# Local attention layers: when GpSimd takes and initialises the value buffers of a tile

## The chip, the cores and the metric

The kernel runs on one core of one Trainium2 chip. The metric is the device time of one execution in microseconds (us), median over several runs. The core has five engines with one queue of instructions each, all in order: TensorE (PE in the profile; PEld is its weight loads), VectorE (DVE), ScalarE (ACT), GpSimd (POOL) and SyncE (SP, which here only issues DMA transfers; its queue is written SPq).

## The reference, cut to what matters

A sequence of blocks works on `x` of 4 x 512 x 128 numbers: cross attentions, mixtures of experts, a feed-forward net, and in the middle a local transformer of six layers. The change lies in the attention of those six layers:

```
for i in range(DEPTH):                                  # DEPTH = 6
    x = attn_layer(shift_tokens(x), Wqkv[i], q_scale[i], k_scale[i], Wo[i]) + x
    x = ffn_layer(shift_tokens(x), ...) + x
# attn_layer: q, k, v = split(x @ Wqkv); 16 heads of 64
#   q = l2norm(q) * qs;  k = l2norm(k) * ksc;  rotary tables on both
#   each window of 32 tokens attends to itself and to the window before it
#   attn = softmax(8 * q k^T, masked);  out = attn @ v;  return out @ Wo
```

The queries and keys are multiplied by the inverse of their norms ("inverse norms" below). The values are not normalised.

## The kernel before, in words

**Tiles and periods.** In `local_transformer` the work is cut into 96 tiles of 128 tokens: 6 layers x 4 sequences (`b`) x 4 tiles (`tt` = 0 to 3). The loop at L2095 runs one period for each `n`. In one period three tiles are worked on at different stages: `T` (number n) gets its queries and keys, their rotation and norms and its values; `T1` (n-1) gets its transposes (`turned`), scores and softmax; `T2` (n-2) gets its probabilities transposed, its average over the values, its output product and its residual. A feed-forward row `F` of the layer is threaded through as well, one quarter per period. The order is written out by hand: the block runs under `manual_schedule`, so each engine executes its instructions in the order of the code; semaphores make it wait where another engine's result is needed.

**GpSimd's queue in one period** is, in order: the sums of the rotation, `rotate` L1865 (four of 128x512, one for each half of the queries and of the keys), with `turned`'s copy of the key edge (L1892, or the memset L1894 at tt = 0) between the second and the third; then `normalise`: L1875, after which ScalarE does a logarithm and an exponential (L1876, L1877), then L1878 to L1881 on 128x32, then L1884, four products of 128x512 with the inverse norms; and then, in `values(T, 0)`, the initialisation of the value buffers L1913, at tt = 0 also L1915 and L1916. In some periods more stands in the queue: two small instructions for the feed-forward's moments (L551, L552), six instructions that build the next layer's tables (L1792, L1798, in the last period of each layer but the last), and two memsets at n = 4 (L527, L528, in `clear`).

**Values.** `values` at L1905 holds two buffers for each tile, `v1` and `v2` (both `v` in the profile), from a pool of three buffers for each name (L1812). Both are 128 x 2 x 8 x 65: 64 numbers for each head, and a 65th column that is one in `v1`, so that the average's product also gives the softmax denominator. GpSimd writes the ones (L1913, 16 numbers per partition). At tt = 0 there is no window before the first, so GpSimd also clears two blocks of 32 partitions of `v2` (L1915, L1916). TensorE multiplies the tokens by the value weights (L1919), and ScalarE copies each half from PSUM to `v1` (L1920, columns 0 to 63). `v2` is `v1` moved by 32 partitions: SyncE issues four DMA copies for each tile (L1922, L1926, L1927, L1928), and two more at tt > 0 which fetch the window before from the previous tile's `v1` (L1924, L1930). These copies move the column of ones too.

`average` (L1980) reads `v1` and `v2` of tile n in period n+2, in two halves g = 0 and 1. So the buffers of tile n-3 have their last reader in period n-1, at `average(T2, 1)`.

Of the kernel before, what the change touches and what calls it, by code (L numbers as in the profile page):

```python
# [21 lines left out]
F32 = mybir.dt.float32  # L22
# [13 lines left out]
DEPTH, LH, LD, WIN = 6, 16, 64, 32  # L36
# [236 lines left out]
def tile_kernel(ctx: ExitStack, tc: tile.TileContext, A: dict, out: bass.AP):  # L273
    nc = tc.nc
    V, G, SC, PE, DMA = nc.vector, nc.gpsimd, nc.scalar, nc.tensor, nc.sync
# [40 lines left out]
    def p_mm(*shape):  # L316
        return psum(shape, "mm", 2)

    def p_tr(*shape):
        return psum(shape, "tr", 2)  # L320
# [199 lines left out]
    def clear(pool, i):  # L520


        t = pool.tile([128, NT, D], F32, name="xn")
        t = t.rearrange("p a b -> p (a b)")[:, : 2 * ROW].rearrange("p (a b) -> p a b", b=ROW)

        def fill(e):
            e.memset(t, 0.0)  # L527
            e.memset(t[:, 1, D + 1 :], NOWHERE)  # L528

        def send(e):  # L530
            for j in (1, 2) if i else (0,):
                r = sent[j].rearrange("(c p) d -> p c d", p=128)
                e.dma_start(r, bc(t[:, int(j != 1)], [128, r.shape[1], ROW], 1))

        def send_back(e):
            r = back[i].rearrange("(c p) d -> p c d", p=128)
            e.dma_start(r, bc(t[:, 0, :D], [128, 2 * NTT, D], 1))

        return fill, send, send_back
# [1211 lines left out]
    def local_columns(i, wp):  # L1751

        W = A["L2_ffn_Wqkv"][i]
        w = []
        for j in range(4):
            t = wp.tile([128, 512], F32, name="wqk", bufs=8)
            DMA.dma_start(t, W[:, 512 * j : 512 * j + 512])
            w.append(t)
        qs = wp.tile([128, 2, LD], F32, name="qs", bufs=1)
        DMA.dma_start(qs[:, 0], A["L2_ffn_q_scale"][i].partition_broadcast(128))  # L1760
        DMA.dma_start(qs[:, 1], A["L2_ffn_k_scale"][i].partition_broadcast(128))
        return w, qs

    def local_weights(i, wp, lf):

        W = A["L2_ffn_Wqkv"][i]
        wv = wp.tile([128, 2, 512], F32, name="wv")
        for x0 in range(2):
            DMA.dma_start(
                wv[:, x0].rearrange("p (k d) -> p k d", d=LD),  # L1770
                W[:, 2 * INNER :].rearrange("p (k x d) -> p x k d", x=2, d=LD)[:, x0],
            )
        wo = wp.tile([128, 8, D], F32, name="wo")
        DMA.dma_start(wo, A["L2_ffn_Wo"][i].rearrange("(c p) d -> p c d", p=128))
        w1 = lf.tile([128, 2 * DI], F32, name="lw1")
        DMA.dma_start(w1, A["L2_ffn_W1"][i])
        w2 = lf.tile([128, 3, D], F32, name="lw2")
        DMA.dma_start(
            w2[:, 0:2], A["L2_ffn_W2"][i][0:256].rearrange("(c p) d -> p c d", p=128)
        )  # L1780
        DMA.dma_start(w2[: CH_W[2], 2], A["L2_ffn_W2"][i][256:DI])
        return wv, wo, w1, w2
# [21 lines left out]
    def local_transformer(Y, lf, lw, columns, tabs):  # L1804

        with ExitStack() as es:
# [5 lines left out]
            vp = es.enter_context(tc.tile_pool(name="lv", bufs=3))  # L1812
# [22 lines left out]
            def queries_or_keys(T, kind, c):  # L1835

                b, tt = T.b, T.tt
                if T.ss is None:
                    T.ss = small.tile([128, 2, LH], F32, name="ss")
                lhs = Y[b][:, 128 * tt : 128 * tt + 128]  # L1840
                t = p_mm(128, 8, LD)
                PE.matmul(t, lhs, T.w[2 * kind + c], start=True, stop=True)  # L1842
                sq = tp.tile([128, 8, LD], F32, name="sq")
                SC.activation(sq, t, AF.Square)  # L1844
                T.raw[kind, c] = t, sq
# [40 lines left out]
            def turned(T, kind):  # L1886
# [15 lines left out]
                else:  # L1902
                    T.qT = t

            def values(T, x0):  # L1905

                b, tt = T.b, T.tt
                if x0 == 0:  # L1910
                    T.v1 = vp.tile([128, 2, LH // 2, LD + 1], F32, name="v1")
                    T.v2 = vp.tile([128, 2, LH // 2, LD + 1], F32, name="v2")
                    G.memset(T.v1[:, :, :, LD : LD + 1], 1.0)  # L1913
                    if tt == 0:
                        G.memset(T.v2[0:32, 0], 0.0)  # L1915
                        G.memset(T.v2[64:96, 1], 0.0)  # L1916
                t = p_tr(128, 8, LD)
                src = Y[b] if x0 == 0 else swapped[b]
                PE.matmul(t, src[:, 128 * tt : 128 * tt + 128], T.wv[:, x0], start=True, stop=True)  # L1919
                SC.copy(T.v1[:, x0, :, 0:LD], t)  # L1920
                if x0 == 0:
                    DMA.dma_start(T.v2[32:128, 0], T.v1[0:96, 0])  # L1922
                    if tt:
                        DMA.dma_start(T.v2[0:32, 0], T.before.v1[96:128, 0])  # L1924
                else:
                    DMA.dma_start(T.v2[96:128, 1], T.v1[64:96, 1])  # L1926
                    DMA.dma_start(T.v2[0:32, 1], T.v1[96:128, 1])  # L1927
                    DMA.dma_start(T.v2[32:64, 1], T.v1[0:32, 1])  # L1928
                    if tt:
                        DMA.dma_start(T.v2[64:96, 1], T.before.v1[32:64, 1])  # L1930
# [36 lines left out]
            def probabilities(T):  # L1967
                T.PT = tp.tile([128, LH // 2, 128], F32, name="PT", bufs=1)
                for g in range(2):
                    SC.copy(T.PT[:, 4 * g : 4 * g + 4], to_features(T.P[:, 4 * g : 4 * g + 4]))  # L1970
# [124 lines left out]
            for n in range(len(tiles) + 2):  # L2095
                T = tiles[n] if n < len(tiles) else None
                T1 = tiles[n - 1] if 0 <= n - 1 < len(tiles) else None
                T2 = tiles[n - 2] if 0 <= n - 2 < len(tiles) else None
                m, phase = divmod(n - 6, 4)
                F = rows[m] if 0 <= m < len(rows) else None  # L2100
                if T:
                    if n % 16 == 7 and T.i + 1 < DEPTH:
                        columns[T.i + 1] = local_columns(T.i + 1, lw)
                        loaded[T.i + 1] = local_weights(T.i + 1, wp, lf)
                    if n == 4:
                        fill, send, send_back = clear(lnp, 1)
                        fill(G)
                        send(DMA)
                        send_back(DMA)
                    if n % 16 == 15 and T.i + 1 < DEPTH:  # L2110
                        tabs[T.i + 1] = local_tables(columns[T.i + 1][1], lw)
                    T.before = tiles[n - 1] if T.tt else None
                    T.w, (T.wv, T.wo) = columns[T.i][0], loaded[T.i][:2]
                    T.tabs = tabs[T.i]
                    queries_or_keys(T, 0, 0)
                if T2:
                    probabilities(T2)
                if T:
                    queries_or_keys(T, 0, 1)
                    rotate(T, 0, 0)  # L2120
                if F:
                    ff_stage(F, phase, False)
                if T2:
                    average(T2, 0)
                if T1:
                    turned(T1, 0)
                if T:
                    queries_or_keys(T, 1, 0)
                if T2:
                    normalised(T2, 0)  # L2130
                if T:
                    rotate(T, 0, 1)
                if T2:
                    average(T2, 1)
                if T1:
                    turned(T1, 1)
                if T:
                    queries_or_keys(T, 1, 1)
                if T2:
                    normalised(T2, 1)  # L2140
                if T:
                    rotate(T, 1, 0)
                if T2:
                    attended(T2)
                if T and T.tt == NT - 1 and n + 1 < len(tiles):
                    swap(tiles[n + 1].b)
                if T1:
                    scores(T1)
                if T:
                    rotate(T, 1, 1)  # L2150
                if T:
                    normalise(T)
                if T1:
                    softmax(T1)
                if T2:
                    project_out(T2)
                    residual(T2)
                if F and phase == 0:
                    ff_norm(F)
                if T:  # L2160
                    values(T, 0)
                    values(T, 1)
                if F:
                    ff_stage(F, phase, True)
# [134 lines left out]
```

## Time and profile before

| | |
|---|---|
| median of 3 runs | 2462.2 us (2459.23 to 2467.07) |
| the profiled execution, its own time | 2456.04 us |
| its span, first to last instruction | 2454.2 us |
| mean granted TensorE clock | 0.953 |
| the 96 local tiles, first query product to last average | 516 to 2165 us |
| busy in the span: PE, DVE, POOL, ACT | 91%, 72%, 55%, 53% |

A timeline row has the start in us, the length in us, the engine, the line, the operation, the names of output and inputs and their shape, how often (consecutive ones are merged, and the length is then of all of them), and in brackets the idle time just before it with what ended it. `issue` as an ender means that the engine waited for nothing the profile shows.

### The profile page before, as it was taken

How to read it: one execution, taken by the hardware profiler on the slowest of the kernel's cores; microseconds unless marked ns; L12 is line 12 of the kernel's file. 1: busy time of each engine (PE TensorE's matmuls, PEld its weight loads, DVE VectorE, ACT ScalarE, POOL GpSimd, SP SyncE). 2: the span in 40 equal slices, each digit the busy share in tenths (PEclk: the TensorE clock that was granted, in tenths of full speed). 3: DMA queues.
4: the chain of work that ended last, by engine and by line, in shares of the span. 5: the costliest groups of instructions: out<-in, count | busy, mean ns of one | idle time of the engine just before them, and what ended most of it. 6: DMA issues, size and time to landing. Idle time of an engine off the chain costs nothing. (4 is left out here: it accounts for less than half of the span.)

```text
span 2454.2 us, 86703 instructions
## 1 busy us (share of the span) xinstructions
PE 2228.0 (91%) x37341; PEld 1479.5 (60%) x37341; DVE 1759.3 (72%) x3896; ACT 1298.1 (53%) x2389; POOL 1338.6 (55%) x1862
## 2 busy tenths in 40 slices
PE   7958969978999999999999999999999999989676
PEld 3536734546666666666666666666666666644355
DVE  5545356866888888777887888887878788767422
ACT  3423325645666655666666666565666666525222
POOL 2141330256667676766667766766667666710433
PEclk9868989988999999999999999999999999989688
DMA  7201110016211121111211121111211111120023
GB/s 182 68 21 41 40 60 2 1 41 135 80 35 29 35 70 36 33 29 35 75 31 36 29 79 33 29 35 27 80 31 31 35 29 35 27 67 23 26 67 95
DMA packets 134298, 116.14 MB, mean 47 GB/s; under 512 B 29506, under 2 KB 102701, under 8 KB 133917
## 3 DMA queue, kind: packets, MB, share of 16 engines
q1 hardware_dynamic: 122037, 99.67, 15.8%
q0 software_dynamic: 4608, 7.35, 0.9%
q8 instruction: 296, 4.85, 0.9%
q10 hardware_dynamic: 7271, 3.58, 0.5%
q14 instruction: 86, 0.70, 0.1%
HBM read 42.84 MB, written 21.52 MB: 26 GB/s over the span
## 5 line engine op out<-in xcount | busy, mean ns | idle before, releaser
L1865 POOL TENSOR_TENSOR rc<-rc,rs 128x512 f32<-128x512 f32 x384 | 489.8, 1276 | 400.7 <-DVE rs L1855 326.3
L1842 PE MATMUL ps_mm<-wqk,y 128*128 128x512 f32 x768 | 397.2, 599 | 5.3 <-issue 3.5
L1884 POOL TENSOR_TENSOR rc<-rc,rn_y 128x512 f32<-128x512 f32 x384 | 388.6, 1044 | 7.5
L1852 DVE TENSOR_TENSOR rc<-ps_mm,tabs 128x512 f32<-128x512 f32 x384 | 262.5, 684 | 129.8 <-ACT sq L1844 126.5
L1844 ACT ACTIVATE sq<-ps_mm 128x512 f32<-128x512 f32 x384 | 231.2, 602 | 161.4 <-PE ps_mm L1842 108.0
L1855 DVE TENSOR_TENSOR rs<-ps_mm,tabs 128x512 f32<-128x512 f32 x384 | 261.5, 681 | 0.2 <-POOL rc L1865 0.2
L1864 DVE TENSOR_REDUCE ss<-sq 128x8 f32<-128x512 f32 x384 | 259.5, 676 | 0.0
L621 PE MATMUL ps_tr<-cst,rc 128*128 128x128 f32 x1536 | 210.9, 280 | 4.3 <-POOL rc L1884 4.0
L1980 PEld LDWEIGHTS ps_av<-v,PT 64*32 64x32 f32 x12288 | 138.1, 105 | 126.5 <-PE ps_tr L621 54.1
L2004 PE MATMUL ps_av<-aT,wo 128*128 128x128 f32 x1536 | 200.7, 283 | 2.4 <-issue 2.4
L2004 PEld LDWEIGHTS ps_av<-aT,wo 128*128 128x128 f32 x1536 | 181.0, 193 | 12.6 <-issue 3.9
L621 PEld LDWEIGHTS ps_tr<-cst,rc 128*128 128x128 f32 x1536 | 165.6, 142 | 24.4 <-POOL rc L1884 5.1
L1949 PE MATMUL ps_sc<-kT,qT 64*32 64x64 f32 x12288 | 148.1, 225 | 33.6 <-issue 32.9
L1980 PE MATMUL ps_av<-v,PT 64*32 64x65 f32 x12288 | 170.3, 225 | 6.2 <-DVE attn L1990 1.7
L1949 PEld LDWEIGHTS ps_sc<-kT,qT 64*32 64x32 f32 x12288 | 141.2, 105 | 44.2 <-issue 38.1
L1056 POOL DMA_INDIRECT back<-ye,to x80 | 78.8, 985 | 147.5 <-DVE ye L1170 104.0
L1842 PEld LDWEIGHTS ps_mm<-wqk,y 128*128 128x128 f32 x768 | 124.5, 192 | 56.3 <-issue 50.1
L1965 ACT ACTIVATE P<-P 128x1024 f32<-128x1024 f32 x96 | 101.4, 1057 | 97.3 <-DVE P L1960 97.3
L1876 ACT ACTIVATE rn_y<-ss 128x32 f32<-128x32 f32 x96 | 22.0, 229 | 237.9 <-POOL ss L1875 237.9
L802 ACT ACTIVATE P<-ps,deltaT 77x512 f32<-77x512 f32 x192 | 115.8, 683 | 56.7 <-PE ps L796 53.0
L1896 ACT COPY qT<-ps_tr 128x512 f32<-128x512 f32 x192 | 103.3, 589 | 74.6 <-PE ps_tr L621 74.3
L1959 DVE TENSOR_REDUCE la_mx<-ps_sc 128x16 f32<-128x1024 f32 x96 | 116.9, 1218 | 31.0 <-PE ps_sc L1949 31.0
(399 smaller groups left out, 4368.9 us busy)
## 6 DMA issues: line engine op xcount, KB each, us to landing
v<-v SPq DMA_DIRECT2D x432, 65.0 KB
v<-v SPq DMA_DIRECT2D x96, 195.0 KB
wqk<-in_L_ffn_Wqkv_dram SPq DMA_DIRECT2D x24, 256.0 KB
sent<-xn SPq DMA_DIRECT2D x2, 2210.0 KB
xe<-sent SPq DMA_DIRECT2D x16, 260.0 KB
back<-xn SPq DMA_DIRECT2D x2, 2048.0 KB
raw<-in_L_ffn_W_dram SPq DMA_DIRECT2D x8, 512.0 KB
w<-in_L_ffn_W_dram SPq DMA_DIRECT2D x16, 256.0 KB
```

The lines of the kernel that those rows point to most:

```text
L621: PE.transpose(t[:, i], src[:, i], ident)
L1842: PE.matmul(t, lhs, T.w[2 * kind + c], start=True, stop=True)
L1844: SC.activation(sq, t, AF.Square)
L1852: V.tensor_tensor(a, t, bc(T.tabs[:, 2 * kind, tt], [128, 8, LD], 1), ALU.mult)
L1855: V.tensor_tensor(r.rearrange("p h (x d) -> p h x d", x=2), t.rearrange("p h (x d) -> p h x d", x=2)[:, :, ::-1], bc(T.tabs[:, 2 * kind + ...
L1864: V.tensor_reduce(T.ss[:, kind, 8 * c : 8 * c + 8], sq, AX.X, ALU.add)
L1865: G.tensor_tensor(a, a, r, ALU.add)
L1884: G.tensor_tensor(a, a, bc(y[:, o : o + 8], [128, 8, LD], 2), ALU.mult)
L1949: PE.matmul(T.banks[32 * w : 32 * w + 32, z, k], T.qT[r, k, 32 * w : 32 * w + 32], T.kT[r, k, 32 * w : 32 * w + 64], start=False, stop=Tru ...
L1959: V.tensor_reduce(mx, T.banks, AX.X, ALU.max)
L1980: PE.matmul(T.means[32 * w : 32 * w + 32, x0, k], T.PT[r, 4 * g + k, 32 * w : 32 * w + 32], (T.v1 if w % 2 else T.v2)[r, x0, 4 * g + k], s ...
L2004: PE.matmul(t, T.wo[:, c], T.aT[:, c], start=(c == 0), stop=(c == 7))
```

## The change

The taking of the two buffers and GpSimd's memsets move out of `values` into a function of their own, called at the start of the tile's period, before its first query product. `values` keeps the product, the copies and the transfers. No instruction is added or taken away.

```
+            def values_open(T):
+                T.v1 = vp.tile([128, 2, LH // 2, LD + 1], F32, name="v1")
+                T.v2 = vp.tile([128, 2, LH // 2, LD + 1], F32, name="v2")
+                G.memset(T.v1[:, :, :, LD : LD + 1], 1.0)
+                if T.tt == 0:
+                    G.memset(T.v2[0:32, 0], 0.0)
+                    G.memset(T.v2[64:96, 1], 0.0)
+
             def values(T, x0):
                 b, tt = T.b, T.tt
-                if x0 == 0:
-                    T.v1 = vp.tile([128, 2, LH // 2, LD + 1], F32, name="v1")
-                    T.v2 = vp.tile([128, 2, LH // 2, LD + 1], F32, name="v2")
-                    G.memset(T.v1[:, :, :, LD : LD + 1], 1.0)
-                    if tt == 0:
-                        G.memset(T.v2[0:32, 0], 0.0)
-                        G.memset(T.v2[64:96, 1], 0.0)
                 t = p_tr(128, 8, LD)
...
                     T.tabs = tabs[T.i]
+                    values_open(T)
                     queries_or_keys(T, 0, 0)
```

## The prediction, made before the changed kernel was built or run

> **What bounds the kernel.** I read the busy times first, then the slices, then the busy times of one stretch of the local layers, then the timeline around the moved memsets, and last who waits for whom.
>
> ```profile
> span 2454.2 us, 86703 instructions
> PE 2228.0 (91%) x37341; PEld 1479.5 (60%) x37341; DVE 1759.3 (72%) x3896; ACT 1298.1 (53%) x2389; POOL 1338.6 (55%) x1862
> ...
> PE   7958969978999999999999999999999999989676
> ```
> ```profile
> 1350.00:1610.00 260.00, 253.68 (x5125) 172.92 (x5124) 213.73 (x375) 160.33 (x295) 178.39 (x252) 1.00 0.16 42
> ```
>
> The columns of the second fence are the stretch, its length, then busy us of PE, PEld, DVE, ACT and POOL, the granted clock, DMA share and GB/s. TensorE is busy 253.68 of 260 us, 97.6%, at full clock; GpSimd 178.39, 69%. So in the local layers, some 1650 of the 2454 us, TensorE sets the time, and a GpSimd edit counts only where TensorE ends up waiting for it. From the memset at 546.57 us to that at 2129.86 there are 93 periods, so one takes 17.03 us.
>
> This is GpSimd and the transfers at the turn from a period with tt = 0 to one with tt = 1, and then one period later (timeline, engines POOL and SP):
>
> ```profile
> 1407.67 3.05 POOL L1884 TENSOR_TENSOR rc<-rc,rn_y 128x512 f32<-128x512 f32 x3
> 1410.65 0.13 POOL L1913 MEMSET v<- 128x16 f32 x1
> 1410.70 0.52 POOL L1915 MEMSET v<- 32x520 f32 x1
> 1411.28 0.53 POOL L1916 MEMSET v<- 32x520 f32 x1
> 1411.88 1.27 POOL L1865 TENSOR_TENSOR rc<-rc,rs 128x512 f32<-128x512 f32 x1
> 1415.03 1.27 POOL L1865 TENSOR_TENSOR rc<-rc,rs 128x512 f32<-128x512 f32 x1 [1.88 <-DVE rs L1855]
> ```
> ```profile
> 1423.33 0.57 ACT L1920 COPY v<-ps_tr 128x512 f32<-128x512 f32 x1
> 1424.17 0.59 ACT L1920 COPY v<-ps_tr 128x512 f32<-128x512 f32 x1 [0.27 <-PE ps_tr L1919]
> 1427.14 0.13 POOL L1913 MEMSET v<- 128x16 f32 x1
> 1427.30 0.53 SPq L1922 DMA_DIRECT2D v<-v  x1
> 1430.42 0.60 SPq L1930 DMA_DIRECT2D v<-v  x1
> ```
>
> Two readings. ScalarE's copies into v1 end at 1424.76, 2.4 us before the memset of the same buffer: they don't wait for it, so no stall of ScalarE is there to remove. What waits is the first transfer, L1922, which carries the ones: it leaves 0.16 us after the memset.
>
> **Part 1, work.** Nothing is added or removed. L1913 is 96 times 128 ns, L1915 and L1916 are 24 times 522 and 525 ns: 12.3 + 25.1 = 37.4 us of GpSimd before and after. The three also keep their slot. Before, the memset of tile n-1 is the last of period n-1, behind the products with the inverse norms; afterwards the memset of tile n is the first of period n, behind the same products and ahead of the same sums. GpSimd sees the same stream with the names one tile on, and in the table-building and clearing periods it passes only those few instructions. Cost 0.
>
> **Part 2, the wait it brings forward.** The memset of tile n must find the buffer of tile n-3 free. At the slot of 1427.14 the last reader, the second half of the average, ran from 1414.54 to 1415.40: 11.7 us earlier. The copies that read the older v1 were issued by 1413.25, 13.9 us earlier. So the wait is met; cost 0. Behind it would stand the first rotation sum, the key edge, and everything of GpSimd's period.
>
> **Part 3, the tt = 0 memsets change periods.** The clears of v2 (1.05 us of rows) move from the start of a tt = 1 period to the start of a tt = 0 period. From L1913 to the first sum it is 1.23 us with them and no wait, and 0.07 without, so I price them at 1.16 us.
> At tt = 1 starts the first sum now begins without a wait in 18 of 23 periods; VectorE's rs was ready at 1411.29 (1410.61 + 0.68), so the sum could start 0.59 us sooner. But the second sum waits 1.88 us for VectorE after it (1.88 to 2.34 in 22 of 23), the third 1.15, the fourth 0.50. What is late next is VectorE in each case; the gain dies there: 0. Without that cover it would be 23 x 0.59 = 13.6 us.
> At tt = 0 starts the added 1.16 us falls in the wait before the first sum, which is 1.37 us or more in 22 of 23 (1.64 or more in 21). In the remaining one (574.8) the next sum waits 0.95 us and the one after 1.17, which takes it up. Cost 0; uncovered, 23 x 1.16 = 26.7 us.
> The trace's who-waits table shows that a late GpSimd sum hardly reaches anyone, and the products behind them reach TensorE only during the filling of the pipeline (530 us):
>
> ```profile
> L1884 POOL TENSOR_TENSOR rc<-rc,rn_y x384: 1039/1044/1086, 529.7 to 2145.9; 128x512 f32<-128x512 f32 x192
> ...
>   PEld ps_tr L621: 5.1, 2
>   PE ps_tr L621: 4.0, 2
> ```
>
> The one to price a GpSimd row by is open to doubt. [...] Rows give 24 x 1.05 = 25.1 us for the clears and spacing 24 x 1.16 = 27.8; as both lie in the cover, the sum is the same by either.
>
> **Part 4, transfers leave earlier.** SyncE's own waits (us, times, longest):
>
> ```profile
> SPq L1922 <- POOL v L1913: 211.4, 70, 7.8
> SPq L1922 <- POOL v L1915: 84.4, 23, 5.5
> ```
> Together 295.8 us on 93 tiles, 3.2 us each. Afterwards L1922 leaves at the first copy's end, about 1424 instead of 1427.3. Their reader is the average two periods on: 1445.83 for this tile, 14.8 us after the last issue ends (1431.02). No row has TensorE waiting for a v2 transfer. Gain 0.
> Behind these copies in SyncE's queue stand the next layer's weight loads (five times, L1757 at 1450.24 right behind L1930's 1449.61), which move about 3 us forward, and once the large clearing transfers (L533 at 579.86, ready since the fill ended at 575.34), which move up to 4.5 us forward. That is no path either, but it bears on a hidden cost: TensorE pauses with the reason "issue", 31 times in L1949 for 32.9 us, with 3.50 us once in L1842 during the clearing transfers. The trace doesn't say what they wait for. Their lengths follow the traffic: beside the weight loads 1.52 (1454.58), elsewhere mostly 0.7 to 1.2. The least seen is 0.69, so between 31 x (0.69 - 1.06) = -11.5 us and 31 x (1.52 - 1.06) = +14.3 us is conceivable. I take 0: L1949 of this period runs at 1436.3, 5.3 us after the last v2 issue ends today and about 8 afterwards, clear of it both times. For the one-off clearing I allow 3 us either way, about its 3.50 pause.
>
> **Part 5, filling the pipeline.** At 533.72 GpSimd is late: memsets and sums run back to back, and TensorE's scores wait 0.66 us for the key edge (L1894). Moving 1.16 us of clears to before 520 us, where GpSimd waits 7.27 us, helps by 0.66 us at most; VectorE is nearly saturated then and had waited only 0.17 us for GpSimd. I take 0.2.
>
> **Sum.** 2456.04 - 0.2 = 2455.8 us for a repeat of the profiled execution. That execution lies 6.2 us below the median, so the forecast is 2462.0. About 0.3% (7.4 us) is what a measurement of this kernel can tell from no change.
>
> **Rivals.**
> A, faster: the earlier first sum at tt = 1 does reach TensorE. 23 x 0.59 = 13.6 us, so 2448.6. For it: 18 of 23 periods have no wait there. Against: the 1.88 us wait behind it, and VectorE waits for a sum once, for 0.2 us. Chance 0.08.
> B, faster: the "issue" pauses shrink as the copies move away from TensorE's dense stretches: 2450.7. For it: they grow with traffic. Against: 5 us of distance already. Chance 0.06.
> C, slower: the same pauses, in L1949 and the averages, grow, because copies and loads now meet whatever TensorE is served by at another moment: up to 14.3 us, 2476.5. It shows from 7.4/31 = 0.24 us for each pause on. For it: 1.52 beside loads. Against: only five loads move. Chance 0.08.
> D, slower: the memset blocks GpSimd's queue, because the buffer counts as free later than I read, say only after the average of the same period (1433.4). That is 6.3 us of stall, less 5.6 us of waits that it displaces (2.46, 1.64, 1.0, 0.5, of this and a like period): 0.7 x 96 = 67 us, 2529. It decides from the displaced 5.6 us on. Against: 11.7 us of margin. Chance 0.04. Nor can the change fail to do what it says: L1922 must lose its wait.
>
> **Numbers.** Forecast 0.74, its own range 2455 to 2470: the runs before spread from 2456.04 to 2467.07, and 3 us for the clearing. The range reaches down to B's 2450.7 and up to 2473, part of C; it leaves out A, D and the rest of C, under 0.2. Faster A + B = 0.14, within 0.3% 0.74, slower C + D = 0.12.
>
> **What would show it.** Right: L1913 in the same slot after L1884 without a wait; SyncE's wait for POOL at L1922 gone, and L1922 within 0.3 us of the first copy; the no-wait first sum at tt = 0 rather than tt = 1; waits before the last sum still 0.50; TensorE 97 to 98% busy between 1350 and 1610; pauses in L1949 near 33 us. Wrong: idle time before L1913 (D), the pauses' sum off by over 7 us (B, C), or a shorter period with the same pauses (A).

## The result, and the profile after

The kernel before took 2462.48 us (median of 14 runs, 2456.51 to 2467.35), the changed one 2473.28 us (median of 14 runs, 2466.56 to 2483.92). The ratio is 1.0048, 95% interval [1.0033, 1.0063]: slower, by 10.8 us between the medians. The forecast was 2462.0 with a range up to 2473.0. The profiled execution of the changed kernel took 2475.07 us. In the changed kernel the lines below the new function are one or more higher: L1922 is now L1923, L1949 is L1950, L2004 is L2005, and the memsets L1913, L1915, L1916 are L1908, L1910, L1911.

First the page of the changed kernel: the span, the busy times, and the group of the scores' products, whose last columns are busy us, mean ns of one, idle us before them and what ended most of it.

```profile
span 2473.2 us, 86773 instructions
...
PE 2236.2 (90%) x37341; PEld 1483.9 (60%) x37341; DVE 1759.7 (71%) x3896; ACT 1299.1 (53%) x2389; POOL 1339.2 (54%) x1862
...
L1950 PE MATMUL ps_sc<-kT,qT 64*32 64x64 f32 x12288 | 148.3, 225 | 40.8 <-issue 40.8
```
The same group on the page of before:
```profile
L1949 PE MATMUL ps_sc<-kT,qT 64*32 64x64 f32 x12288 | 148.1, 225 | 33.6 <-issue 32.9
```

VectorE, ScalarE and GpSimd are busy for as long as before, within 1 us. What grew is TensorE's idle time with the reason "issue" in the scores, from 32.9 us to 40.8, and its busy time by 8.2 us, with the same 37341 products.

Now the turn from tt = 0 to tt = 1 in the timeline after (engines POOL, ACT and SP), the place that the prediction showed:

```profile
1403.32 4.05 POOL L1884 TENSOR_TENSOR rc<-rc,rn_y 128x512 f32<-128x512 f32 x4
1407.31 0.13 POOL L1908 MEMSET v<- 128x16 f32 x1
1407.36 0.52 POOL L1910 MEMSET v<- 32x520 f32 x1
1407.93 0.53 POOL L1911 MEMSET v<- 32x520 f32 x1
1409.11 1.28 POOL L1865 TENSOR_TENSOR rc<-rc,rs 128x512 f32<-128x512 f32 x1 [0.65 <-DVE rs L1855]
...
1419.96 1.05 ACT L1921 COPY v<-ps_tr 128x512 f32<-128x512 f32 x2
1420.59 0.53 SPq L1923 DMA_DIRECT2D v<-v  x1
1422.45 0.58 SPq L1929 DMA_DIRECT2D v<-v  x1
1423.78 0.13 POOL L1908 MEMSET v<- 128x16 f32 x1
```

GpSimd runs as forecast: the memset stands in the same slot behind L1884, without a wait; the clears now stand ahead of a tile with tt = 0, and the first sum behind them still has 0.65 us to spare. The transfer L1923 leaves as soon as the first copy into `v1` is done (about 1420.5; the row of 1419.96 merges both copies), 3.2 us ahead of the next memset instead of 0.16 us behind one. In SyncE's own waits the two rows for POOL's memsets (211.4 and 84.4 us) are gone, and the row for ScalarE's copy has grown. Before, then after:

```profile
SPq L1922 <- ACT v L1920: 911.2, 89, 12.4
```
```profile
SPq L1923 <- ACT v L1921: 1224.8, 95, 15.3
```

So where do 10.8 us come from? I took one mark in each period, the start of ScalarE's logarithm L1876, in both profiled executions, and subtracted. Over the 96 tiles the changed kernel loses 12.3 us (1648.38 to 1660.67 us from the first query product to the last average), and nearly all of it in four steps: +4.9 us from tile 7 to 8, +2.5 from 23 to 24, +1.6 from 39 to 40, +3.5 from 71 to 72 (and -0.2 from 55 to 56). In between the difference wanders by about 1 us and comes back, apart from 4 to 5 us lost at tile 5 and regained at tile 6, beside the clearing transfers. Those five are the periods with `n % 16 == 7`, in which SyncE issues the next layer's weight loads (L1757 to L1781, 2.6 MB). The two executions differ by another 4.0 us ahead of the first local tile and 2.8 us behind the last, in code that the change leaves alone.

Period 7 in the timelines, SP's first load and TensorE's scores and output product. Before:

```profile
635.91 2.86 SPq L1757 DMA_DIRECT2D wqk<-in_L_ffn_Wqkv_dram  x4
637.54 1.05 PE L1949 MATMUL ps_sc<-kT,qT 64*32 64x64 f32 x84
639.55 0.68 PE L1949 MATMUL ps_sc<-kT,qT 64*32 64x64 f32 x44 [0.97 <-issue]
640.16 2.05 PE L2004 MATMUL ps_av<-aT,wo 128*128 128x128 f32 x16
```
After:
```profile
635.35 2.96 SPq L1757 DMA_DIRECT2D wqk<-in_L_ffn_Wqkv_dram  x4
641.17 1.05 PE L1950 MATMUL ps_sc<-kT,qT 64*32 64x64 f32 x84
645.38 0.93 PE L1950 MATMUL ps_sc<-kT,qT 64*32 64x64 f32 x44 [3.16 <-issue]
646.24 3.78 PE L2005 MATMUL ps_av<-aT,wo 128*128 128x128 f32 x16
```

The reader is to see three things. The loads started 1.6 us ahead of the scores before, and start 5.8 us ahead of them now. The pause comes behind the same 84th product in both kernels, and grows from 0.97 to 3.16 us. And the 16 products behind the long pause take 3.78 us instead of 2.05. The pauses beside the five loads were 0.97, none, 1.08, 1.52 and 0.90 us, and are 3.16, 2.43, 2.61, 1.34 and 2.55 (with another 0.78 just before it); the output product of the first and of the last is slow (3.78, 3.63).

The busy times of the 10 us around that pause, before and then after (columns as in the prediction; the granted clock is the third from the end):

```profile
636.00:646.00 10.00, 9.03 (x172) 6.11 (x171) 6.33 (x10) 6.06 (x11) 7.46 (x12) 1.00 0.77 209
```
```profile
641.00:651.00 10.00, 6.84 (x155) 5.93 (x155) 4.90 (x8) 2.82 (x6) 8.43 (x14) 0.66 0.70 173
```

The clock was full before and averages 0.66 after: the granted clock is 1.00 up to 644.25 us, inside the pause, and 0.50 from there to 651.08. What TensorE waits for in the pause, the trace's DMA packets show. The DMA view lists a queue of kind "instruction" (q8) with 296 packets and 4.85 MB, 16 KB each; 37341 products and 37341 weight loads over 296 packets are 252 instructions for each packet, and 256 with the 1107 semaphore and drain instructions that the trace has on TensorE's queue. So a packet holds one block of 256 instructions, and an edge is where a block ends. Counted in such blocks, all 32 pauses in the scores after, and 30 of the 31 before, stand at one and the same place, an edge; from one to the next there are 378, 630, 1009 or 1637 products and the like, multiples of 126 within one. And packets and edges keep step: the last packet of q8 to start ahead of a pause's end is the 45th in period 7 and the 129th in period 39, 84 packets for 84 blocks, and so in all these 62 pauses. Each of them ends 2.2 to 3.1 us after that packet has started and 1.2 to 1.6 us after it has ended. So I read the pause as TensorE's wait for the packet. In the microsecond in which such a packet falls beside these scores, 636 to 637 before and 642 to 643 after, the queues read:

```profile
q1 hardware_dynamic: 84, 0.11, 45.6%
q8 instruction: 1, 0.02, 6.7%
```
```profile
q1 hardware_dynamic: 879, 0.23, 99.1%
q8 instruction: 1, 0.02, 6.0%
```

Before, the packet came ahead of the scores, at 636.89, and the DMA engines were half idle; after, it came inside the pause, at 642.78, with 879 packets of the loads in the same microsecond. Its own transfer is no longer than before (0.96 us, before 1.06). It starts later: 1.69 us ahead of the pause before, 0.56 us into the pause after. In the other three pauses of over 2 us beside the loads in the changed kernel the packet starts between 0.38 us ahead and 0.24 us behind the start of the pause, where the pauses away from loads and clearing have it 0.9 to 1.9 us ahead.

### The profile page after: what moved, and what is told of

It reads as the page before. It is cut to its first block, busy times and chain, and to the rows that moved or that the text cites. A ratio compares the mean times of both kernels' runs of the same rounds, so it can differ in the third digit from the quotient of the medians.

```text
span 2473.2 us, 86773 instructions
## 1 busy us (share of the span) xinstructions
PE 2236.2 (90%) x37341; PEld 1483.9 (60%) x37341; DVE 1759.7 (71%) x3896; ACT 1299.1 (53%) x2389; POOL 1339.2 (54%) x1862
## 3 DMA queue, kind: packets, MB, share of 16 engines
q1 hardware_dynamic: 122037, 99.67, 15.8%
q8 instruction: 296, 4.85, 0.8%
## 5 line engine op out<-in xcount | busy, mean ns | idle before, releaser
L1842 PE MATMUL ps_mm<-wqk,y 128*128 128x512 f32 x768 | 396.1, 598 | 5.4 <-issue 3.2
L1884 POOL TENSOR_TENSOR rc<-rc,rn_y 128x512 f32<-128x512 f32 x384 | 388.6, 1044 | 7.5
L2005 PE MATMUL ps_av<-aT,wo 128*128 128x128 f32 x1536 | 204.0, 286 | 3.1 <-issue 2.9
L2005 PEld LDWEIGHTS ps_av<-aT,wo 128*128 128x128 f32 x1536 | 184.1, 195 | 13.4 <-issue 4.8
L1950 PE MATMUL ps_sc<-kT,qT 64*32 64x64 f32 x12288 | 148.3, 225 | 40.8 <-issue 40.8
L621 PEld LDWEIGHTS ps_tr<-cst,rc 128*128 128x128 f32 x1536 | 165.2, 141 | 25.6 <-POOL rc L1884 5.1
L1950 PEld LDWEIGHTS ps_sc<-kT,qT 64*32 64x32 f32 x12288 | 141.2, 105 | 51.4 <-issue 46.2
L1842 PEld LDWEIGHTS ps_mm<-wqk,y 128*128 128x128 f32 x768 | 124.4, 192 | 55.8 <-issue 49.5
L1876 ACT ACTIVATE rn_y<-ss 128x32 f32<-128x32 f32 x96 | 22.0, 229 | 235.4 <-POOL ss L1875 235.4
```

The source lines that it names most:

```text
L621: PE.transpose(t[:, i], src[:, i], ident)
L1884: G.tensor_tensor(a, a, bc(y[:, o : o + 8], [128, 8, LD], 2), ALU.mult)
L1950: PE.matmul(T.banks[32 * w : 32 * w + 32, z, k], T.qT[r, k, 32 * w : 32 * w + 32], T.kT[r, k, 32 * w : 32 * w + 64], start=False, stop=Tru ...
L2005: PE.matmul(t, T.wo[:, c], T.aT[:, c], start=(c == 0), stop=(c == 7))
```

## The experiments

Theory **L**: the value copies leave about 3 us earlier, so the loads queued behind them on SyncE leave earlier in their period (3.6 to 4.6 us further ahead of the scores in the five), their traffic meets the fetch of TensorE's next instruction block in the scores, and TensorE pauses. Against it stood **V**, the value copies of all 96 tiles disturb TensorE at their new place, and **G**, GpSimd's stream delays something in every period. The time of one kernel differs from chip to chip (the kernel before had medians of 2409.71, 2457.76, 2422.3 and 2422.91 us beside these runs), so each ratio is against the kernel before on the same chip.

**Only the five tiles whose copies stand ahead of the loads, and only the others.** The first kernel opens only tiles with `n % 16 == 6` early, the second all but those (`!=` and `==` exchanged). The others are opened where the kernel before does it. A sixth tile, n = 86, falls under the condition too, with no loads behind it, so the second kernel opens 90 tiles early, not 91:

```
-                    values_open(T)
+                    if n % 16 == 6:
+                        values_open(T)
...
+                    if n % 16 != 6:
+                        values_open(T)
```

> The value buffers are opened early only for the five tiles in front of a weight load (n mod 16 = 6); the other 91 are opened late, as before. Theory L (the change moves the next layer's weight loads some 4 us ahead in their period, and TensorE's pause in the scores beside them grows): the whole slowdown stays, 1.0048 of before (1.003 to 1.006), with pauses of 2.4 to 3.2 us in the scores of periods 7, 23, 39 and 71. Rival V (the earlier v copies cost something in each of the 96 tiles): 5/96 of the slowdown, 1.0003. Rival G (the clears' new place in GpSimd's queue, all at tt = 0): none of these five tiles has clears, so 1.000.

> The reverse: buffers opened early for all tiles but those five. L: the loads leave as late as before, so 1.000 (0.9985 to 1.0015), no pause over 1.6 us in the scores beside the loads. V: 91/96 of the slowdown, 1.0045. G: all clears are moved, so 1.0048.

Measured: 1.0054 [1.0034, 1.0074] for the five alone, 0.9992 [0.9976, 1.0007] for the others. Five tiles carry the whole cost, and 90 cost nothing that could be measured; V and G fall as causes of it. The pauses beside the loads are 1.20, 3.79, 0.82, 3.41 and 2.54 us with the five, and 1.27, 2.42, none, none and 0.63 with the others. That the long ones would be those of periods 7, 23, 39 and 71 was wrong: 7 and 39 stay short, and 55 is long. The 2.42 misses what I had expected of it (none over 1.6): a long pause can happen at the old start too, only less often. Period 23 with the five, TensorE's timeline:

```profile
887.30 0.77 PE L1950 MATMUL ps_sc<-kT,qT 64*32 64x64 f32 x40 [3.79 <-issue]
888.00 3.47 PE L2005 MATMUL ps_av<-aT,wo 128*128 128x128 f32 x16
```

**The change, with the loads held back to about their old start.** A 16-byte transfer that needs the period's second rotation sum stands ahead of them in SyncE's queue, and their calls move behind that sum's:

```
-                    if n % 16 == 7 and T.i + 1 < DEPTH:
-                        columns[T.i + 1] = local_columns(T.i + 1, lw)
-                        loaded[T.i + 1] = local_weights(T.i + 1, wp, lf)
...
                     rotate(T, 0, 1)
+                    if n % 16 == 7 and T.i + 1 < DEPTH:
+                        gate = small.tile([1, 4], F32, name="gate")
+                        DMA.dma_start(gate, T.rot[0, 1][0:1, 0, 0:4])
+                        columns[T.i + 1] = local_columns(T.i + 1, lw)
+                        loaded[T.i + 1] = local_weights(T.i + 1, wp, lf)
```

> The changed kernel, all 96 tiles early, but the weight loads are held in SyncE's queue by a transfer of 16 bytes that waits for the second rotation sum of their period, about 4.5 us after the memset's slot, where they left before the change. L: 1.000 (0.9985 to 1.0015), pauses beside the loads about 1 us again. V and G: 1.0048, since every copy and every memset is where the change put it.

Measured: 0.9989 [0.9971, 1.0007]; pauses 1.02, 0.69, none, 0.98, 1.18. The loads start 0.9 us ahead of the scores in period 7 (1.6 before the change). With all of the change in place but the loads' start put back, the cost is gone. In a third kernel the loads wait for the row maxima of the period's scores, and so leave behind the scores:

> The changed kernel with the weight loads held until the row maxima of the scores are found, so that they leave behind the scores of their period and are over before the next scores, some 13 us later. L: no pause over 1.3 us in the scores of periods 7, 23, 39, 55, 71 or of the period after each, 0.997 to 1.000 of before. If it is not the place in the period but any load traffic that costs: pauses elsewhere (averages, output product) of together some 2 us per load, 1.003 to 1.005.

Measured: 1.0004 [0.9987, 1.0022], no pause over 1.3 us beside the loads. Moving them behind the scores wins nothing over the old start.

**No loads at all**, in the changed kernel and in the kernel before. All layers then use the first layer's weights:

```
-                        columns[T.i + 1] = local_columns(T.i + 1, lw)
-                        loaded[T.i + 1] = local_weights(T.i + 1, wp, lf)
+                        columns[T.i + 1] = columns[0]
+                        loaded[T.i + 1] = loaded[0]
```

> The changed kernel without the weight loads of layers 1 to 5: all six layers use the weights of layer 0, so this part of the result is another one. To be read beside the kernel before with the same loads left out. L: no pause over 1.3 us in the scores of those periods, and within 3 us of its counterpart; against the kernel before with loads about 0.998 to 1.000 (the pauses of 0.9 to 1.5 us beside loads may lose a few tenths each). V and G: still 11 us over its counterpart, 1.003 to 1.005 against before.

> The kernel before with the weight loads of layers 1 to 5 left out (all layers use the weights of layer 0, so this part of the result is another one). Counterpart of e4, which was at 0.9987 of before (0.9971 to 1.0003). L: the same as e4 within its interval, 0.997 to 1.000. V and G: 0.0045 below e4, about 0.994.

Measured: 0.9987 [0.9971, 1.0003] for the changed kernel, 0.9996 [0.9979, 1.0012] for the one before. Without the loads no difference is left between the two that these intervals could tell.

**Which part of the loads?** The value weights are fetched in pieces of 256 bytes, and I suspected their many small packets. One kernel leaves them out in the changed kernel (later layers use the first layer's); another is the kernel before with `local_weights` called ahead of `local_columns`, so that the small pieces come first:

> The changed kernel without the loads of the value weights (2 of the 10 transfers of a layer, 0.5 MB in pieces of 256 bytes; layer 0's are used in all layers, so this part of the result is another one). In the changed kernel these were in flight when the scores began, before the change the query and key weights in pieces of 2 KB were. If the small pieces are what delays TensorE: pauses beside the loads about 1 us, 0.999 to 1.001. If any traffic at that point does: still 2 us and more in most, 1.003 to 1.005.

> The kernel before, with only the order of the loads changed: value and output weights first, query and key weights behind them; they start where they did before the change. If the small pieces are to blame, they are now in flight at the scores: pauses of 2 us and more, 1.002 to 1.005. If the start of the loads in the period decides, whatever they are: as before, 0.999 to 1.001.

Measured: 1.0075 [1.0052, 1.0098] without the value weights, 0.9999 [0.9979, 1.0020] with the order swapped. The suspicion falls: without the small pieces the pauses are 3.71, 1.13, 3.55, 3.69 and 3.36 us, four of the five longer than with them. With the order swapped, the loads that meet the scores are others and the start is the old one, and no cost is measured, though one pause of the five is 2.06 us, with a slow output product behind it (3.39); the others are 1.38, 0.69, 1.06 and 1.63. So the small pieces are not needed for the cost; the start relative to the scores is what the slower kernels have in common. Whether the kind of the pieces changes the length of a pause is not shown. Period 7 without the value weights:

```profile
626.86 0.93 PE L1952 MATMUL ps_sc<-kT,qT 64*32 64x64 f32 x44 [3.71 <-issue]
627.71 3.78 PE L2007 MATMUL ps_av<-aT,wo 128*128 128x128 f32 x16
```

**Is it TensorE's instruction stream?** If a pause is the wait for the next block of instructions, it stands at a fixed place of the program, and 20 more instruction pairs ahead of it must move it by 20 products. The edit, ahead of the local loop, first in one run of the changed kernel and then timed in both:

```
+            extra = p_tr(128, NT, 128)
+            for j in range(20):
+                PE.transpose(extra[:, j % NT], ident, ident)
             for n in range(len(tiles) + 2):
```

> The changed kernel with 20 more transposes on TensorE ahead of the local loop (40 instructions with their weight loads; nothing reads them). It asks what the pauses wait for. If TensorE waits for its own next block of instructions, the pause sits at a fixed count of instructions, so every one moves 20 matmuls earlier: in period 7 from behind the 84th score product to behind the 64th, in period 71 from behind the 100th to behind the 80th. If the pause comes of a wait for data, it stays where it was.

> The kernel before with 20 additional transposes of 128x128 ahead of the local loop, whose output nobody reads; together they take about 2 us. If TensorE's pauses come at fixed places of its instruction stream, they lie 20 matmuls earlier than in the kernel before, and some that fell into the scores vanish, as in the look at the changed kernel with the same transposes (26 pauses, 23.2 us): then 0.994 to 1.000 in spite of the 2 us. If only the moment counts, the pauses stay behind the same matmul and the time is 1.001.

> The changed kernel with the same 20 transposes, now timed. If the loads' start relative to the scores is the whole cause, and the place in the stream does not matter, it stays 4 to 7 parts in 1000 above the kernel before with the transposes. If the pause needs both the loads and a block edge late in the scores, the difference between the two shrinks to what the periods with an edge there cost: under 0.003, since the pause of period 7 (the largest, 4.9 us of the 12) was gone in the one look.

Measured in the one run: 2406.54 us, without an interval. The pauses moved by 19 products where they stayed: behind the 91st instead of the 110th in period 5, the 81st instead of the 100th in period 71, the 83rd instead of the 102nd in period 79. Others vanished, among them period 7's; 26 were left with 23.2 us in all.

Timed: 0.9963 [0.9940, 0.9985] for the kernel before with the transposes, 0.9954 [0.9936, 0.9973] for the changed one. The first gained 9 us from work that nobody needs (4.5 us ahead of the loop, at a granted clock of 0.50, where about 2 us had been expected); its pauses in the scores are 25 with 25.6 us instead of 31 with 32.9. And the ratio between the two is 0.9999 (2412.59 to 2412.77; resampling the 10 runs of each gives 0.9976 to 1.0022): with the stream shifted, **the change shows no cost**, within some 5 us either way, though the loads start early, 5.0 us ahead of the scores in period 7. TensorE's timeline there:

```profile
624.69 0.84 PE L1950 MATMUL ps_sc<-kT,qT 64*32 64x64 f32 x63 [1.36 <-issue]
625.46 2.05 PE L2005 MATMUL ps_av<-aT,wo 128*128 128x128 f32 x16
```

63 products are left behind the pause instead of 44, and it is 1.36 us. Three of the other four load periods have no pause over 0.2 us; the fifth has 2.93, with the slow output product behind it (3.50).

Where the edges fall explains this, and the two first traces already show it. Counted in blocks of 256, there are 96 edges in the scores of the local layers, in both kernels. 63 of them lie behind the 82nd product of their 128 or earlier: none of these has a pause before, and one after (the one of period 4 below). 33 lie behind the 84th or later: 30 of these have a pause before and 31 after. The edges of periods 7, 23, 39, 55 and 71 lie behind the 84th, 88th, 92nd, 96th and 100th product, all among the late ones; with the 20 transposes they lie behind the 65th, 69th, 73rd, 77th and 81st, and only the last has the long pause. So beside the loads it took two things together: dense traffic during the scores, and the edge of an instruction block late in them. That an edge must lie late is no rule: in period 4 of the changed kernel, beside the clearing transfers, the edge behind the 56th product has a pause of 3.35 us.

**A version that beats both.** If pauses come from traffic that meets block edges, thin traffic should shorten the long ones in either kernel. Here each layer's loads go out in eight portions, one in each of eight periods, and the clearing transfers that stood together in period 4 in 26 portions over many periods (`later` puts portion j of a layer's loads into `late[n + j]`):

```
-                        columns[T.i + 1] = local_columns(T.i + 1, lw)
-                        loaded[T.i + 1] = local_weights(T.i + 1, wp, lf)
+                        later(T.i + 1, n)
...
-                        send(DMA)
-                        send_back(DMA)
...
+                    for dst, src in late.pop(n, ()):
+                        DMA.dma_start(dst, src)
```

> The changed kernel with the traffic thinned out: the weight loads go in eight portions of 256 to 600 KB, one at the start of each of eight periods, and the 6.4 MB that clear the tables for the last block go in 26 portions of about 270 KB, one per period, rather than in one block in period 4. L and what it says of the clearing (pauses of 3.5 and 2.2 us and slower products behind them in periods 4 to 6): no pause over 1.5 us in the whole local part, the four periods from 4 on 5 to 7 us shorter, 0.996 to 0.998 of before. V and G: 1.002 or more.

> The kernel before with the same thinned traffic. L: the change itself is then worth nothing, so the same as e8 within 0.001. V and G: 0.0045 faster than e8.

> The changed kernel with thin traffic (loads over eight periods, clearing in 26 portions) and the 20 transposes. If the gain of thin traffic (0.9962) and that of the shift are the same pauses, it comes out at 0.994 to 0.997; if they add, at 0.988 to 0.993.

Measured: the changed kernel 0.9962 [0.9946, 0.9978], the kernel before 0.9973 [0.9956, 0.9989], both with thin traffic; the changed one with thin traffic and the 20 transposes 0.9898 [0.9876, 0.9920], 27 us between its median and that of the kernel before on that chip. The two gains add up, as far as the intervals tell (0.9962 x 0.9963 = 0.9925). The four periods 4 to 7, which hold the clearing and the first loads, take 63.5 us (changed) and 63.2 us (before) with thin traffic, against 74.6 in the kernel before and 79.0 in the changed one; that is 11 us less than before, where 5 to 7 had been expected. In the changed kernel no pause over 1.5 us is left in the local part. In the kernel before with thin traffic one of 2.15 us stands in period 23, with a slow output product (3.55), and the pauses in its scores come to 34.9 us, no less than the 32.9 of the kernel before: what its profiled execution, one of the slowest of its twelve, gains lies in the four periods alone. The group of the scores with both edits:

```profile
L1950 PE MATMUL ps_sc<-kT,qT 64*32 64x64 f32 x12288 | 145.2, 225 | 19.0 <-issue 19.0
```

19.0 us of pauses are left, of 40.8; even there they don't go away.

## Why the prediction was wrong

Point by point, by its own steps.

- **Bound**, right: TensorE sets the time; the loss is TensorE's.
- **Part 1, work, and Part 2, the wait brought forward**, right: same slot, no wait. Rival D had no ground.
- **Part 3, the clears change periods**, right: the first sum at tt = 0 keeps a reserve (0.65 us at 1409.11), and the wait ahead of the last sum is still 0.50 us. Rival A's 13.6 us did not come. The sign that the prediction listed, a first sum without a wait at tt = 0, did not come either (0.65 us of wait is left); it did not follow from the 1.37 us or more of wait that the same part found there.
- **Part 5, filling**: the marks gain 0.3 us at tiles 2 and 3, for 0.2 forecast. That is less than the 1 us by which they wander, so it neither confirms the size nor contradicts it.
- **Part 4, transfers leave earlier**, is the step that failed: its term of 0 for the "issue" pauses. It saw the loads move and took the pauses to follow the traffic, and then took 0, since the scores at 1436.3 lie clear of the last copy. That looked at the copies of a tile, in a period without loads. In a period with loads the distance that matters is from the loads to the scores, 1.6 us before in period 7 and 5.8 after. At 1.6 us the packet with the next block started 1.0 us behind the first load, with the DMA engines at 45.6%; at 5.8 us it started 7.4 us behind the first load, with the engines at 99.1%, and the pause grew by 2.19 us. Two readings of the trace before were wrong as well. That the trace does not say what the pauses wait for: its instruction packets tell it, in the scores for 30 of the 31. And that their lengths follow the traffic rested on one row, 1.52 us: the other load periods had 0.97, none, 1.08 and 0.90, and the 1.50 us of period 10 had no load beside it.
- **Rival C** named the right mechanism, and mis-sized it. It spread the price over 31 pauses, 0.46 us each, and called "only five loads move" a reason against. Five were enough: their pauses grew by 2.19, 2.43, 1.53, -0.18 and 1.65 us, 7.6 us together, and the clock that drops after two of them adds 1.73 and 1.58 us in the output product. Together that is 10.9 us, beside 12.3 in the marks and 10.8 in the medians. The sign that the prediction set for C came too: the sum of the pauses is off by 7.9 us. The row to price a pause beside dense traffic by was the 3.50 us in L1842 during the clearing, which the prediction quoted but kept for the clearing alone. The 0.97 to 1.52 us beside the loads were taken at the loads' old start.
- **Range and chances.** 5 x (3.50 - 1.06) = 12.2 us would have been C's price by that row, 2474.2, with five moved loads as its condition; 0.08 was too small a chance for it.

The trace before held what was needed: 296 packets of 16 KB on TensorE's instruction queue, 256 instructions to each, 30 of the 31 pauses in the scores at the end of such a block, and the row of 3.50 us, at the end of a block as well. Of the 96 block edges in the scores, 30 had a pause before and 32 after. A reader who starts from these would ask of each moved transfer whether it meets a stretch in which TensorE uses up a block quickly; 128 score products and as many weight loads, a whole block, take 1.46 us here where no pause breaks them.

What stays open: what decides the length of one pause in one execution. With the same early loads the one at n = 55 is 1.34 us in the changed kernel's profile and 3.41 with the five tiles alone, the one at n = 7 is 3.16 and 1.20, the one at n = 39 is 2.61 and 0.82. The traces show that an edge early in the scores mostly has no pause and a late one has, but not why, nor what holds a packet back before it starts; that it queues behind the loads' packets is a guess that no run shows.

## What to carry to other kernels

When an edit lets a queue run earlier, look at what stands behind the moved transfers on that queue, in the few periods in which something large does, and measure the distance from that to the densest stretch of small TensorE instructions. Pauses of TensorE with the reason "issue" which stand behind the same instruction in every execution were block edges here (62 of the 63 in the scores of the two kernels), and the times of the instruction packets tell; thin out the transfers beside them, and try moving the edges by a few instructions before concluding that an edit is worth or costs half a percent.

## What the runs showed of the hardware

- TensorE's instructions came in 296 packets of 16 KB on one DMA queue (q8, 4.85 MB), which the page counts in a share of the same 16 DMA engines as the data's queue (0.9% and 15.8% of the span before). TensorE resumed 2.2 to 3.1 us after a packet's start in all 62 pauses at block edges in the scores of the two kernels. Beside 2.6 MB of loads that had started 5.5 to 6.2 us ahead of the scores, a pause of the changed kernel was 1.3 to 3.2 us long; away from loads and clearing, 0.5 to 1.5.
- Twenty idle transposes in front of a loop changed the time of the whole kernel by -0.37% (0.9963 [0.9940, 0.9985]), and the difference between two versions of it from +0.48% to -0.01% (-0.24 to +0.22).
- The clock after a pause was no matter of its length alone. In the changed kernel the granted clock went to 0.50 inside the pause of 3.16 us (from 644.25 us on, for 6.83 us) and behind the one of 2.55 (from 1743.34, for 3.41), and stayed at 1.00 behind those of 2.43 and 2.61. I took 17 pauses of over 2 us in the scores from nine profiled executions, the changed kernel's and those of eight experiments, all with products at full speed ahead of them, and the 16 output products behind them (2.05 us at full clock). The eight from 2.92 us on have slow products behind them (2.77 to 3.78 us); of the nine between 2.06 and 2.61 us four do (3.09 to 3.63), the one of 2.06 among them, and five have products of 2.05. Two more don't count, since the clock was low ahead of them: the one of 2.19 in the kernel before (0.50 from 596.77 to 610.42 us), and one of 3.40 with the order of the loads swapped, ahead of which 110 score products took 1.82 us (1.31 at the same place with the 90 tiles opened early).
